# A graph layer's edge stages moved two pairs closer to their sums, with the third term of x1 . sh1 on ScalarE

## The chip, the core and the metric

The kernel runs on one core of a Trainium2 chip. The core has five engines with a queue each, worked off in order: TensorE (PE, matmuls; its weight loads are listed as PEld), VectorE (DVE), ScalarE (ACT), GpSimd (POOL) and SyncE (SP). They run side by side and meet through semaphores; POOL and SP here mostly issue DMA transfers. The metric is the time of one execution on the device, in microseconds (us); lower is better.

## The reference

A layer norm, a graph network, linear attention and a mixture of experts follow each other on 3125 nodes of width 512, all in float32. The change lies in the graph network, in what is done for each of 50,000 edges. A node's row is one scalar part of 128 channels (x0) and a vector part of 128 channels by 3 (x1). Cut to that:

```python
ip1 = jnp.einsum('eum,eum->eu', p1[edge_dst], p1[edge_src]) / 3.0
s0 = jnp.concatenate([pd0, pd0, ip1], axis=-1)
w = ssp(edge_attr @ W_f1) @ W_f2 * (ssp(s0 @ W_s1) @ W_s2)
w1, w2, w3, w4 = jnp.split(w, 4, axis=-1)
x0e, x1e = split_irreps(x[edge_src])
sh0, sh1 = (edge_sh[:, 0], edge_sh[:, 1:4])
out0 = w1 * x0e * sh0[:, None] + w4 * (jnp.einsum('eum,em->eu', x1e, sh1) / jnp.sqrt(3.0))
out1 = w2[:, :, None] * x0e[:, :, None] * sh1[:, None, :] + w3[:, :, None] * x1e * sh0[:, None, None]
out = jax.ops.segment_sum(merge_irreps(out0, out1), edge_dst, num_segments=N)
```

`ssp` is softplus less log 2. The einsum `eum,em->eu` is the x1 . sh1 of the title: a sum of three products, one for each component of the edge's direction.

## The kernel before, in words

First the kernel sorts the edges: each gets a record of 48 words (`recs`: its four sh values, source, destination, destination within its tile of 128 nodes, and the already known half of the hidden layer), laid out so that edges of one destination tile stand together. Node rows are written to two tables, `rows_d` (for the destination) and `rows_s` (for the source).

Then comes the edge stage, `run_pairs`. 128 edges are a tile, two tiles a pair, four tiles a quad (G = 4). 212 pairs, 106 quads, are always run; a further run follows only if the edges need more pairs. The stage's steps, with the lines that the profile names:

- `fetch` (POOL): per pair two gathers of `gd` (L710) and two of `gx` (L714). At the first pair of a quad SP loads the quad's records `rec2` (L699). There are 3 buffers of `gd`, 5 of `gx`, 6 of `rec2`, each holding a quad.
- `products` (DVE, L726): gd times gx for one pair, in two halves of a quad's `prod`.
- `turn` (PE, L734): 12 transposes that add up the three components of a quad into the PSUM tile `ps_ip`; `turn2` (ACT, L743) copies it to `ip`.
- `hidden` (PE): 24 small matmuls into `ps_h`, eight each from the records (L750), from `gd` (L755) and from `ip` (L760).
- `softplus` (ACT, L768, L771, L774, and L777 which copies the other half of `hT`), `softplus2` (DVE, L781, the second half of `hT`).
- `weigh`: for one pair PE makes `wa` (L799) and `wb` (L803) from the two halves of `hT`; ACT scales and copies `wa` to `wt` (L806 twice, L809); DVE multiplies by `wb` (L810). `wa` and `wb` have one buffer each.
- `dots` (ACT, L820) and `dots2` (DVE, L828 and L830): x1 . sh1 of a pair.
- `which` (DVE, L840): a matrix `one` that is 1 where an edge belongs to a node of the tile.
- `feats`: the edge's features `ft`: DVE L858, then six ACT instructions (L865) that scale one of its results, DVE L869, and DVE L874, which uses the dot product.
- `gather_up` (PE, L882): one.T times ft, added up over the pair in PSUM (eight matmuls in the profile); `keep_sums` (DVE, L891) adds it to the node tile's sums in `acc`.

POOL also copies a matrix of the experts' weights (`line_up`, L898) every sixth pair.

The order on PE, ACT, DVE and POOL is the program's own (`tc.manual_schedule`): what `run_pairs` writes down first stands first in that engine's queue, and waits there. The loop body is one pass for pair s. `due(a)` gives the quad whose first pair is s + a, so a step called with it comes in every second pass. `fetch` stands LEAD pairs ahead, `products` 7 and 6 ahead of the quad's first pair, `turn` 5, `hidden` 4, `softplus` 3, `softplus2` 2; `weigh`, `feats` and `dots2` work for pair s + 1, `dots` for s + 2, `gather_up` for s, `keep_sums` for s - 1. Most tiles that pass between the engines have two buffers, `ps_ip` and `ps_h` one.

Of the kernel before, what the change touches and what calls it, by code (L numbers as in the profile page):

```python
# [8 lines left out]
F32 = mybir.dt.float32  # L9
I32 = mybir.dt.int32  # L10
AF = mybir.ActivationFunctionType
ALU = mybir.AluOpType
# [4 lines left out]
P = 128  # L17
D = 512
MUL = 128
PR = 2  # L20
# [23 lines left out]
def gnn_mix_moe_kernel(ctx: ExitStack, tc: tile.TileContext, a: dict, out: bass.AP):  # L44
# [5 lines left out]
    nc = tc.nc  # L50
# [72 lines left out]
    with ExitStack() as c1:  # L123
# [313 lines left out]
        work = c1.enter_context(tc.tile_pool(name="work1", bufs=2, reuse_waits="tile"))  # L437
# [18 lines left out]
        for k0 in range(0, NPR, 44):  # L456
            ks = slice(k0, min(NPR, k0 + 44))
            k = ks.stop - k0
# [207 lines left out]
    with ExitStack() as c2:  # L666
        w = c2.enter_context(tc.tile_pool(name="w2", bufs=1, reuse_waits="tile"))
        gat = c2.enter_context(tc.tile_pool(name="gat", bufs=4, reuse_waits="tile"))
        work = c2.enter_context(tc.tile_pool(name="work2", bufs=2, reuse_waits="tile"))
# [24 lines left out]
        def fetch(q, k):  # L694

            Q = quads[q]
            if k == 0:
                Q.rec = gat.tile([P, G, REC], F32, name="rec2", bufs=6)
                loaded = nc.sync.dma_start(  # L699
                    Q.rec, recs[q * G * P : (q + 1) * G * P, :].rearrange("(p i) f -> p i f", i=G)  # L700
                )
                if q == 0:
                    for put in placed:
                        waits_for(loaded, put)

                Q.gd = gat.tile([P, G, HID + 3 * MUL], F32, name="gd", bufs=3)
                Q.gx = gat.tile([P, G, 3 * MUL + D], F32, name="gx", bufs=5)
            reci = Q.rec.bitcast(I32)
            for i in (2 * k, 2 * k + 1):
                nc.gpsimd.indirect_dma_start(  # L710
                    out=Q.gd[:, (i + 2) % G, :], out_offset=None, in_=rows_d[:, :],
                    in_offset=bass.IndirectOffsetOnAxis(ap=reci[:, i, 5:6], axis=0),
                )
                Q.last = nc.gpsimd.indirect_dma_start(  # L714
                    out=Q.gx[:, i, :], out_offset=None, in_=rows_s[:, :],
                    in_offset=bass.IndirectOffsetOnAxis(ap=reci[:, i, 4:5], axis=0),
                )

        def products(q, k):

            Q = quads[q]
            if k == 0:
                Q.prod = work.tile([P, G, 3 * MUL], F32, name="prod")
            x = slice(2 * k, 2 * k + 2)
            d = slice(2 - 2 * k, 4 - 2 * k)
            nc.vector.tensor_mul(Q.prod[:, d, :], Q.gd[:, d, HID:], Q.gx[:, x, : 3 * MUL])  # L726
# [13 lines left out]
        def turn2(q):  # L740
            Q = quads[q]
            Q.ip = work.tile([P, G, P], F32, name="ip")
            nc.scalar.copy(Q.ip, Q.ps_ip)  # L743
# [21 lines left out]
        def softplus(q):  # L765
            Q = quads[q]
            sp = work.tile([P, P], F32, name="sp")
            nc.scalar.activation(sp, Q.ps[:, 1, :], AF.Abs)  # L768
            if q * PR < NPR_MOST:
                with tc.issue_after(table.ins):  # L770
                    nc.scalar.activation(sp, sp, AF.Exp, scale=-1.0)  # L771
            else:
                nc.scalar.activation(sp, sp, AF.Exp, scale=-1.0)
            nc.scalar.activation(sp, sp, AF.Ln, bias=half, scale=0.5)  # L774
            Q.sp = sp
            Q.hT = work.tile([P, 2, P], F32, name="hT")
            nc.scalar.copy(Q.hT[:, 0, :], Q.ps[:, 0, :])  # L777

        def softplus2(q):
            Q = quads[q]  # L780
            nc.vector.scalar_tensor_tensor(  # L781
                Q.hT[:, 1, :], Q.ps[:, 1, :], 0.0, Q.sp, op0=ALU.max, op1=ALU.add
            )
# [3 lines left out]
        def parts(s):  # L787

            return quads[s // 2], (s % 2 * 2, s % 2 * 2 + 1)

        def weigh(s):

            Q, tiles = parts(s)
            R = pairs[s]
            wa = ps_w.tile([P, PR, D], F32, name="wa")
            wb = ps_w.tile([P, PR, D], F32, name="wb")
            for k, i in enumerate(tiles):
                r = slice(i * HID, (i + 1) * HID)
                nc.tensor.matmul(wa[:, k, :], Q.hT[r, 0, :], w_f2[r, :], start=True, stop=True)  # L799
            for k, i in enumerate(tiles):  # L800
                i = (i + 2) % G
                r = slice(i * HID, (i + 1) * HID)
                nc.tensor.matmul(wb[:, k, :], Q.hT[r, 1, :], w_s2[r, :], start=True, stop=True)  # L803
            R.wt = work.tile([P, PR, D], F32, name="wt")
            for k, i in enumerate(tiles):
                nc.scalar.activation(  # L806
                    R.wt[:, k, : 2 * MUL], wa[:, k, : 2 * MUL], AF.Copy, scale=Q.rec[:, i, 0:1]
                )
            nc.scalar.copy(R.wt[:, :, 2 * MUL :], wa[:, :, 2 * MUL :])  # L809
            nc.vector.tensor_mul(R.wt, R.wt, wb)  # L810

        def dots(s):

            Q, tiles = parts(s)
            R = pairs[s]
            R.dot = work.tile([P, 2, PR, MUL], F32, name="dot")
            x = Q.gx[:, :, 3 * MUL :]
            for c in (1, 2):
                for k, i in enumerate(tiles):
                    nc.scalar.activation(  # L820
                        R.dot[:, c - 1, k, :], x[:, i, c * MUL : (c + 1) * MUL], AF.Copy, scale=Q.rec[:, i, c : c + 1]
                    )

        def dots2(s):
            Q, tiles = parts(s)
            R = pairs[s]
            x = Q.gx[:, :, 3 * MUL :]
            nc.vector.tensor_add(R.dot[:, 0], R.dot[:, 0], R.dot[:, 1])  # L828
            for k, i in enumerate(tiles):
                nc.vector.scalar_tensor_tensor(  # L830
                    R.dot[:, 0, k, :], x[:, i, 3 * MUL :], Q.rec[:, i, 3:4], R.dot[:, 0, k, :],
                    op0=ALU.mult, op1=ALU.add,
                )

        def which(s):

            Q, tiles = parts(s)
            R = pairs[s]
            R.one = work.tile([P, PR, P], F32, name="one")
            nc.vector.tensor_tensor(  # L840
                R.one, lane.unsqueeze(1).to_broadcast([P, PR, P]),
                Q.rec[:, tiles[0] : tiles[1] + 1, 6:7].to_broadcast([P, PR, P]), op=ALU.is_equal,
            )
# [52 lines left out]
        def line_up(e, l):  # L896
            src = a["Wh"][e, l] if l < NL else a["Wo"][e]
            nc.gpsimd.dma_start(  # L898
                w_rows[l][e * P : (e + 1) * P, :].rearrange("p (k f) -> p k f", k=4),
                src.rearrange("(k p) f -> p k f", p=P),  # L900
            )

        def run_pairs(lo, hi):

            with tc.manual_schedule(
                engines={
                    mybir.EngineType.PE, mybir.EngineType.Activation, mybir.EngineType.DVE, mybir.EngineType.Pool
                }
            ):
                LEAD = 9  # L910
                for s in range(lo - LEAD, hi):
                    def due(ahead):

                        q, r = divmod(s + ahead, PR)
                        return [q] if r == 0 and lo <= q * PR < hi else []

                    if s + LEAD < hi:
                        fetch((s + LEAD) // PR, (s + LEAD) % PR)
                    if s >= lo and s % 6 == 0 and mats:
                        line_up(*mats.pop(0))  # L920
                    for q in due(2):
                        softplus2(q)
                    if lo <= s + 1 < hi:
                        which(s + 1)
                        dots2(s + 1)
                    for k in range(2):
                        for q in due(7 - k):
                            products(q, k)
                    if lo <= s - 1:
                        keep_sums(s - 1)  # L930
                    if lo <= s + 1 < hi:
                        weigh(s + 1)
                    for q in due(3):
                        softplus(q)
                    for q in due(5):
                        turn(q)
                    if lo <= s + 2 < hi:
                        dots(s + 2)
                    if lo <= s + 1 < hi:
                        feats(s + 1)  # L940
                    for q in due(5):
                        turn2(q)
                    if lo <= s:
                        gather_up(s)
                    for q in due(4):
                        hidden(q)
                keep_sums(hi - 1)

# [14 lines left out]
    with ExitStack() as c3:  # L963
# [17 lines left out]
        with tc.tile_pool(name="work3", bufs=2) as work:  # L981
# [107 lines left out]
            tiles = w.tile([P, NE], F32, name="tiles")  # L1089
# [308 lines left out]
```

## Time and profile before

| what | value |
|---|---|
| time, median of 3 runs | 2830.79 us (2830.1 to 2841.89) |
| the profiled execution: time / span | 2827.58 us / 2825.7 us |
| mean granted TensorE clock | 0.951 |
| busy share of the span: PE, PEld, DVE, ACT, POOL | 87%, 55%, 65%, 50%, 63% |
| first gather of the edge stage (L710) | 610.47 us |
| first L810 / first L882 | 651.58 us / 654.85 us |
| last L891 | 1913.47 us |

The profile is one execution. Its page gives each engine's busy time over the whole span; an average over stages with different limits. The edge stage takes about 1300 of the 2826 us, so the same shares are read again for a stretch inside it. In the timeline a line is a start in us, a duration, an engine and a source line; in brackets stands how long the engine had been idle and who released it. Instructions of one engine can overlap by a little, so the distance from one start to the next is what an instruction costs its queue.

### The profile page before, as it was taken

The numbers are of one execution on the slowest core, as the hardware profiler recorded it, in microseconds if no ns is written. First come the engines' busy times: TensorE is split into PE (matmuls) and PEld (weight loads), VectorE is DVE, ScalarE is ACT, GpSimd is POOL, SyncE is SP. The second block draws the span as 40 slices with busy tenths as digits, with TensorE's granted clock in tenths as the row PEclk, the third lists the DMA queues.
The fourth block names the chain that finished last, engine by engine and source line by source line (L and its number), as shares of the span: only waits on it lengthen the run. The fifth ranks groups of instructions, "written<-read, shape, count | busy, mean of one in ns | idle before, by whom it ended". The sixth has DMA issues, their size and how long they took to land. (4 is left out here: it accounts for less than half of the span.)

```text
span 2825.7 us, 45347 instructions
## 1 busy us (share of the span) xinstructions
PE 2472.2 (87%) x15014; PEld 1561.5 (55%) x15014; DVE 1838.4 (65%) x3758; ACT 1426.0 (50%) x4077; POOL 1771.1 (63%) x1756
## 2 busy tenths in 40 slices
PE   2676999208999999999999999996599999999998
PEld 2453466204444444444444444445488888888887
DVE  5878322028999999999999999995522222222222
ACT  1463321007888888888888888882311111111111
POOL 1778777777777777777777777721355555555553
PEclk7898999658999999999999999999799999999999
DMA  6663156338888888888888888835722723966452
GB/s 258 214 205 117 38 193 222 101 106 278 267 264 252 275 262 265 260 262 264 264 264 265 264 264 264 250 99 178 300 76 72 243 71 108 332 244 228 143 200 95
DMA packets 191656, 588.29 MB, mean 208 GB/s; under 512 B 54405, under 2 KB 79418, under 8 KB 179384
## 3 DMA queue, kind: packets, MB, share of 16 engines
q0 software_dynamic: 135216, 496.50, 54.3%
q1 hardware_dynamic: 49864, 82.54, 8.9%
q10 hardware_dynamic: 6336, 6.28, 0.7%
q8 instruction: 123, 2.02, 0.3%
q14 instruction: 117, 0.96, 0.1%
HBM read 635.54 MB, written 119.53 MB: 267 GB/s over the span
## 5 line engine op out<-in xcount | busy, mean ns | idle before, releaser
L882 PE MATMUL ps_s<-ft,one 128*128 128x512 f32 x1696 | 776.1, 600 | 40.5 <-DVE ft L869 40.5
L710 POOL DMA_INDIRECT gd<-rows_d,rec x424 | 460.1, 1085 | 181.4 <-issue 94.8
L882 PEld LDWEIGHTS ps_s<-ft,one 128*128 128x128 f32 x1696 | 306.0, 190 | 436.6 <-issue 256.0
L714 POOL DMA_INDIRECT gx<-rows_s,rec x424 | 416.4, 982 | 173.8 <-issue 96.3
L865 ACT ACTIVATE ft<-ft,rec 128x128 f32<-128x128 f32 x1272 | 395.0, 389 | 205.2 <-DVE ft L858 205.2
L396 POOL DMA_INDIRECT recs<-again,at_i x392 | 411.3, 1049 | 134.8 <-issue 108.8
L1273 ACT ACTIVATE h<-ps_f,bias 128x128 f32<-128x128 f32 x318 | 116.7, 367 | 622.0 <-PE ps_f L1260 611.9
L1260 PE MATMUL ps_f<-h,we 128*128 128x128 f32 x3392 | 401.6, 277 | 0.4 <-DVE h L1275 0.2
L1275 DVE TENSOR_SCALAR h<-ps_f,bias 128x128 f32<-128x128 f32 x318 | 111.1, 350 | 435.7 <-PE ps_f L1260 431.7
L1260 PEld LDWEIGHTS ps_f<-h,we 128*128 128x128 f32 x3392 | 387.0, 192 | 2.2 <-DVE h L1275 0.4
L1187 POOL DMA_INDIRECT we<-w_rows,w_at x212 | 214.5, 1012 | 225.8 <-PE ps_y L1291 99.5
L820 ACT ACTIVATE dot<-gx,rec 128x128 f32<-128x128 f32 x848 | 271.6, 397 | 0.0
L734 PE MATMUL ps_ip<-ident,prod 128*128 128x128 f32 x1272 | 165.9, 281 | 118.7 <-DVE prod L726 118.7
L810 DVE TENSOR_TENSOR wt<-wt,wb 128x1024 f32<-128x1024 f32 x212 | 257.0, 1212 | 0.3 <-ACT wt L809 0.3
L734 PEld LDWEIGHTS ps_ip<-ident,prod 128*128 128x128 f32 x1272 | 140.3, 143 | 198.5 <-issue 198.5
L803 PE MATMUL wb<-w_s,hT 32*128 32x512 f32 x848 | 240.3, 643 | 3.1 <-DVE wt L810 3.1
L799 PE MATMUL wa<-w_f,hT 32*128 32x512 f32 x848 | 239.4, 641 | 0.0
L726 DVE TENSOR_TENSOR prod<-gd,gx 128x768 f32<-128x768 f32 x212 | 201.6, 951 | 22.6 <-DMA gx<-rows_s,rec 22.6
L1260 PEld LDWEIGHTS ps_f<-xt,we 128*128 128x128 f32 x1696 | 200.0, 194 | 26.0 <-issue 23.7
L869 DVE TENSOR_TENSOR ft<-gx,wt 128x768 f32<-128x768 f32 x212 | 205.2, 968 | 0.0
L1260 PE MATMUL ps_f<-xt,we 128*128 128x128 f32 x1696 | 200.4, 277 | 0.7 <-ACT xt L1208 0.7
L1291 PE MATMUL ps_y<-we,h 128*128 128x512 f32 x424 | 196.1, 605 | 0.0
(301 smaller groups left out, 3545.6 us busy)
## 6 DMA issues: line engine op xcount, KB each, us to landing
w_rows<-in_Wh POOLq DMA_DIRECT2D x24, 1024.0 KB
rows_s<-r SPq DMA_DIRECT2D x24, 448.0 KB
recs<-zero POOLq DMA_DIRECT2D x10, 1056.0 KB
rec<-recs SPq DMA_DIRECT2D x106, 96.0 KB
lined<-rec SPq DMA_DIRECT2D x14, 672.0 KB
again<-lined POOLq DMA_DIRECT2D x14, 672.0 KB
w_rows<-in_Wo POOLq DMA_DIRECT2D x8, 1024.0 KB
gd<-rows_d,rec POOLq DMA_INDIRECT x424
```

What stands on the lines that cost most here:

```text
L396: put = nc.gpsimd.indirect_dma_start(out=recs[:, :], out_offset=bass.IndirectOffsetOnAxis(ap=at_i[:, t : t + 1], axis=0), in_=again[c][:, ...
L710: nc.gpsimd.indirect_dma_start(out=Q.gd[:, (i + 2) % G, :], out_offset=None, in_=rows_d[:, :], in_offset=bass.IndirectOffsetOnAxis(ap=reci ...
L714: Q.last = nc.gpsimd.indirect_dma_start(out=Q.gx[:, i, :], out_offset=None, in_=rows_s[:, :], in_offset=bass.IndirectOffsetOnAxis(ap=reci[ ...
L734: nc.tensor.matmul(ps[:, i, :], Q.prod[:, i, b * P : (b + 1) * P], ident, is_transpose=True, start=(b == 0), stop=(b == 2),)
L799: nc.tensor.matmul(wa[:, k, :], Q.hT[r, 0, :], w_f2[r, :], start=True, stop=True)
L803: nc.tensor.matmul(wb[:, k, :], Q.hT[r, 1, :], w_s2[r, :], start=True, stop=True)
L810: nc.vector.tensor_mul(R.wt, R.wt, wb)
L820: nc.scalar.activation(R.dot[:, c - 1, k, :], x[:, i, c * MUL : (c + 1) * MUL], AF.Copy, scale=Q.rec[:, i, c : c + 1])
L865: nc.scalar.activation(R.ft[:, k, D + c * MUL : D + (c + 1) * MUL], R.ft[:, k, 2 * D :], AF.Copy, scale=Q.rec[:, i, c : c + 1],)
L882: nc.tensor.matmul(R.ps, R.one[:, k, :], R.ft[:, k, m * D : (m + 1) * D], start=(k == 0 and m == 0), stop=(k == 1 and m == 1),)
L1187: nc.gpsimd.indirect_dma_start(out=dst, out_offset=None, in_=src, in_offset=bass.IndirectOffsetOnAxis(ap=at[:, j : j + 1], axis=0), bounds ...
L1260: nc.tensor.matmul(pss[f], ws[l][:, k, f * P : (f + 1) * P], h[:, k, :], start=(k == 0), stop=(k == 3))
```

## The change

Two edits, both in the edge stage.

First, the third product of x1 . sh1. `dots` lets ACT write all three products (six instructions a pair instead of four) into a `dot` tile with room for three, and `dots2` is two DVE additions over the pair instead of one addition and two multiply-adds.

Second, the order in `run_pairs`. LEAD goes from 9 to 7. `products` comes 5 and 4 pairs ahead of the quad's first pair (was 7 and 6), `turn` and `turn2` 3 (was 5), `hidden` 3 (was 4), `softplus` 2 (was 3). `softplus2` stays in the pass 2 ahead and goes from the head of the pass to behind `feats`; `softplus` now stands ahead of `turn`. `hidden` and `turn2` of a quad are now in one pass.

```diff
-            R.dot = work.tile([P, 2, PR, MUL], F32, name="dot")
+            R.dot = work.tile([P, 3, PR, MUL], F32, name="dot")
             x = Q.gx[:, :, 3 * MUL :]
-            for c in (1, 2):
+            for c in (1, 2, 3):
...
         def dots2(s):
-            Q, tiles = parts(s)
             R = pairs[s]
-            x = Q.gx[:, :, 3 * MUL :]
             nc.vector.tensor_add(R.dot[:, 0], R.dot[:, 0], R.dot[:, 1])
-            for k, i in enumerate(tiles):
-                nc.vector.scalar_tensor_tensor(
-                    R.dot[:, 0, k, :], x[:, i, 3 * MUL :], Q.rec[:, i, 3:4], R.dot[:, 0, k, :],
-                    op0=ALU.mult, op1=ALU.add,
-                )
+            nc.vector.tensor_add(R.dot[:, 0], R.dot[:, 0], R.dot[:, 2])
...
-                LEAD = 9
+                LEAD = 7
...
                         fetch((s + LEAD) // PR, (s + LEAD) % PR)
                     if s >= lo and s % 6 == 0 and mats:
                         line_up(*mats.pop(0))
-                    for q in due(2):
-                        softplus2(q)
                     if lo <= s + 1 < hi:
                         which(s + 1)
                         dots2(s + 1)
                     for k in range(2):
-                        for q in due(7 - k):
+                        for q in due(5 - k):
                             products(q, k)
                     if lo <= s - 1:
                         keep_sums(s - 1)
                     if lo <= s + 1 < hi:
                         weigh(s + 1)
+                    for q in due(2):
+                        softplus(q)
                     for q in due(3):
-                        softplus(q)
-                    for q in due(5):
                         turn(q)
                     if lo <= s + 2 < hi:
                         dots(s + 2)
                     if lo <= s + 1 < hi:
                         feats(s + 1)
-                    for q in due(5):
+                    for q in due(2):
+                        softplus2(q)
+                    for q in due(3):
                         turn2(q)
                     if lo <= s:
                         gather_up(s)
-                    for q in due(4):
+                    for q in due(3):
                         hidden(q)
```

## The prediction

> **What bounds the kernel now.** Three views, in this order. First the busy time of each engine by stretch (PE, PEld, DVE, ACT, POOL in us of 200, then the granted clock and the DMA share), for a stretch in the middle of the edge stage:
>
> ```profile
> 1300.00:1500.00 200.00, 193.85 (x1147) 90.50 (x1145) 197.65 (x353) 167.32 (x521) 143.38 (x141) 1.00 0.84 266
> ```
>
> VectorE (DVE) is busy 99%, TensorE (PE) 97% at full clock, ScalarE (ACT) 84%. Every stretch from 700 to 1900 us reads alike: 212 pairs, 106 quads, run in one rhythm. Second the timeline of that rhythm (start, duration, engine, line, what):
>
> ```profile
> 1303.29 0.40 PE L760 MATMUL ps_h<-ip,w_s1c 128*32 128x128 f32 x8
> 1303.62 0.70 PE L799 MATMUL wa<-w_f,hT 32*128 32x512 f32 x2
> ...
> 1306.12 0.81 ACT L806 ACTIVATE wt<-wa,rec 128x256 f32<-128x256 f32 x2
> 1306.83 0.57 ACT L809 COPY wt<-wa 128x512 f32<-128x512 f32 x1
> ...
> 1309.47 0.69 DVE L858 TENSOR_TENSOR ft<-wt,gx 128x512 f32<-128x512 f32 x1
> 1310.19 1.86 ACT L865 ACTIVATE ft<-ft,rec 128x128 f32<-128x128 f32 x6 [0.52 <-DVE ft L858]
> 1310.99 0.41 DVE L874 TENSOR_TENSOR ft<-wt,dot 128x256 f32<-128x256 f32 x1
> 1311.12 3.70 PE L882 MATMUL ps_s<-ft,one 128*128 128x512 f32 x8 [0.39 <-DVE ft L869]
> 1311.33 0.28 DVE L781 SCALAR_TENSOR_TENSOR hT<-ps_h,sp 128x128 f32<-128x128 f32 x1
> 1311.53 0.41 DVE L840 TENSOR_TENSOR one<-lane,rec 128x256 f32<-128x256 f32 x1
> 1311.86 0.41 DVE L828 TENSOR_TENSOR dot<-dot 128x256 f32<-128x256 f32 x1
> 1311.96 0.56 ACT L743 COPY ip<-ps_ip 128x512 f32<-128x512 f32 x1
> 1312.31 0.61 DVE L830 SCALAR_TENSOR_TENSOR dot<-gx,rec,dot 128x128 f32<-128x128 f32 x2
> 1312.84 0.95 DVE L726 TENSOR_TENSOR prod<-gd,gx 128x768 f32<-128x768 f32 x1
> 1313.71 0.68 DVE L891 TENSOR_TENSOR acc<-acc,ps_s 128x512 f32 x1
> 1314.31 1.21 DVE L810 TENSOR_TENSOR wt<-wt,wb 128x1024 f32<-128x1024 f32 x1
> 1315.55 0.69 DVE L858 TENSOR_TENSOR ft<-wt,gx 128x512 f32<-128x512 f32 x1
> 1316.16 0.95 DVE L869 TENSOR_TENSOR ft<-gx,wt 128x768 f32<-128x768 f32 x1
> 1317.03 0.41 DVE L874 TENSOR_TENSOR ft<-wt,dot 128x256 f32<-128x256 f32 x1
> ```
>
> DVE has no bracket of idle time on any line: it goes from one instruction to the next. Its L781 comes again at 1323.25, so a quad costs 11.92 us, and PE, ACT and POOL wait for DVE. Third, the end of the stage, where L726 has run out and DVE is relieved of 0.87 us a pair:
>
> ```profile
> 1871.59 3.70 PE L882 MATMUL ps_s<-ft,one 128*128 128x512 f32 x8 [0.34 <-DVE ft L869]
> ...
> 1883.07 3.70 PE L882 MATMUL ps_s<-ft,one 128*128 128x512 f32 x8
> ```
>
> The same matmuls, a quad apart, now without a wait: PE's own limit is 11.48 us.
>
> **The change, part by part.** I use start-to-start times, since neighbouring instructions overlap by some 0.07 us.
>
> *The third term.* On DVE the two L830 (0.53 from the first of them to L726) give way to one add of 128x256. Its nearest row is L840 (0.33 to the next) or L828, which is followed by an instruction that needs it (0.45); 0.33, because L726 follows and doesn't need it. DVE saves 0.20 a pair: 11.93 - 0.40 = 11.53 a quad, against PE's 11.48. ACT gets two more L820 a pair at 0.295 (six L865 start within 1.77), 1.18 a quad; it idles 1.38 + 0.52 = 1.90 now. Alone this would bring about 0.40 x 106 = 42 us.
>
> The Trainium skill ("Perfetto Trace Analysis", Identifying the Most-Contended Engine) says to optimize the engine of highest occupancy first. DVE's 99% agrees, and by that rule the sum would be 2827.6 - 42 = 2786 us. The rule doesn't ask what the new order makes each queue wait for, and the rows below speak against it.
>
> *The order.* What follows weighs more. Call the pass in which L734 (turn) is issued odd, the other even. In the new order PE's odd queue is L799/L803 (weights of the next pair), L734, L882, then L750, L755, L760 (hidden). L760 needs L743 of the same pass, which stands last on ACT: behind L806, L809, six L820 and six L865. Today L760 uses a copy made a pass earlier. In the even pass L781 now stands last on DVE, and the next L803 on PE needs it; today it is first, a pass ahead of its use. So all three queues form one ring per quad, which I walk with the rows above:
>
> 1. DVE from L781 to L810: 0.20 (to L840), 0.33, 0.45 (L828), 0.33 (new add), 0.87 (L726), 0.60 (L891) = 2.78
> 2. L810 to L858 1.24; L858 to the first L865 0.73; six L865 1.77 until L743 starts
> 3. L743 to L760: 0.67. The copy lasts 0.56; in the fill, at a lower clock, it starts at 627.54, L760's weights load at 628.18 and its matmuls start at 628.29, so between 0.64 and 0.75
> 4. L760 to L799 0.33 (1303.29 to 1303.62); L799 to L806 1.17 (661.34 to 662.51, where ACT waits for it); L806 to L809 0.71; L809 to L810 0.62 (663.24 to 663.86, where DVE waits for it)
> 5. L810 to L858 1.24, to L869 0.61, to L874 0.87, to L781 0.34
>
> The ring: 2.78 + 3.74 + 0.67 + 2.83 + 3.06 = 13.08 us a quad, 1.15 more than today's 11.93. For 106 quads +122 us. Queued behind the waiting L760 are the next L799 and L882; behind the waiting L803 the odd L734 and L882. PE's odd pass doesn't cover it: from L799 it has 1.08 of its own, 1.37 of L734, 3.53 of L882 and 0.46 of L750 and L755 (1303.62, 1304.70, 1306.07 and 1309.60 in the timeline; 1302.83 to 1303.29), 6.44, while L799 to the end of L743 needs 1.17 + 0.71 + 0.62 + 1.24 + 0.73 + 1.77 + 0.56 = 6.80. Nor is anything left to do between L882 and the late L803 of the odd pass.
>
> In the even pass ACT has a second route from L809 to L810 through softplus (1.57 with L809), six L820 (1.77), six L865 (1.77), L806 and L809 (1.33) = 6.44, against 6.46 over DVE. So of the third term's saving nothing more is to be had: ACT is level.
>
> *The lead.* Gathers start seven pairs ahead and L726 stands two pairs nearer, so gather to L726 stays two pairs; in the fill a gather lands some 3.4 us after its issue, well within 13. On POOL eight gathers at about 1.3 are 10.4 us a quad, L898's transfers 0.4: it keeps up. Buffers (three gd, five gx, six rec2) come free earlier relative to their gathers; POOL's present waits for L810 and L865 and SP's loads of rec2 hold nobody. If that cover went, a late landing would stall L726 for its lateness: today's six such stalls are all in the fill, 22.6 us together. The fill gets shorter: the first L810 comes after L726 of the fifth pair instead of the seventh, which started at 639.38 and 650.70, -11 us. At the end fewer passes run without L726: +1.
>
> *Sum*, against the profiled execution (span 2825.7, 1.9 around it, 2827.6 in all): +122 - 11 + 1 = +112, 2939.6. The median shown is 3.2 above that execution: 2943.
>
> *Bounds.* Below: step hand-overs cost nothing beyond the instructions themselves (0.11 in step 3, 0.04 to 0.05 at three others), 12.83 a quad, and the fill saves 15: 2827.6 + 95 - 15 + 3 = 2911. Above: all 24 hidden matmuls wait, not the last eight (0.80 instead of 0.33, the rows from L750 to L799), the new add costs 0.45, ACT adds 0.06: 13.73 a quad, +191, the fill saves 6: 3016. I take 13.08, as each of its steps has a row of its own.
>
> **The rivals.** *The ring is open and the DVE cut shows (other side).* If L743 found ACT free before the six L865, or L760's wait were covered, the ring would fall under DVE's 11.53. For it: DVE at 99%, and PE already idles for DVE. Against it: queues run in order and the deficit of 0.36 (6.80 against 6.44) and the late L803 recur in every quad. It decides from the point where the ring loses 1.15, as by the 1.77 of the L865. Price: -42 - 11 + 3 gives 2777.
>
> *The clock falls.* PE would idle 13.08 - 11.48 = 1.6 us a quad, 12%. From 130 to 160 us it was busy 77% at a clock of 0.83; there a quad would cost at least 11.48 / 0.83 = 13.8, over 3018. Against it: from 190 to 250 us 81% busy at 1.00, from 1930 to 1970 us 68% at 1.00. The low clocks stand beside long pauses.
>
> *The edits cancel.* A ring of 11.93 gives 2820 to 2830; nothing in the rows makes it so.
>
> **How the numbers follow.** The ring as walked has 0.87, the open ring 0.06, cancelling 0.02, a lower clock or a longer ring above 3015 0.05. The predicted time is the first's, 2943, and the range is its bounds with some room, 2900 to 3015; 1.3 in 10 is left out. The runs of before spread by 0.4%, so about 0.5% is what can be told from no change. Faster 0.06, same 0.02, slower 0.92.
>
> **What would show it.** In the middle of the stage a quad of 13.1 us; PE waiting at L760 for ACT L743, some 0.4 us a quad, and at L803 for DVE L781, some 1.2 us (together the 1.6 above); DVE waiting at L810 for ACT L809 once a quad, about 1 us; DVE busy about 11.53 / 13.08 = 88%; clock still 1.00; the first L810 about 11 us earlier. Wrong if L760 shows no wait, if DVE stays at 99%, or if PE's clock drops.

## The result and the profile after

The changed kernel takes 2957.77 us (median of 4 runs, 2953.07 to 2960.25) against 2835.84 us before (4 runs): a ratio of 1.0431 with a 95% interval of 1.0411 to 1.0452. It is 4.3% slower. The prediction was 2943 us in a range of 2900 to 3015. The profiled execution took 2959.99 us (span 2958.2 us), 132.4 us more than the one before.

The middle of the edge stage, busy time by stretch (PE, PEld, DVE, ACT, POOL, then clock, DMA share, GB/s):

```profile
1300.00:1500.00 200.00, 194.03 (x1027) 85.11 (x1025) 175.43 (x287) 169.59 (x533) 131.48 (x128) 1.00 0.76 238
```

DVE has fallen from 197.65 to 175.43 us of 200 (88%, the figure predicted). No engine has come nearer to being full in its place: ACT is busy 169.59 us (167.32 before), the clock is full, and the DMA share is lower. PE reads 97% as before although it does less (1027 matmuls instead of 1147 in the same 200 us); the timeline tells why. Line numbers past L826 are 5 to 6 lower in the new file: L865 is now L859, L858 L852, L869 L863, L874 L868, L882 L876, L840 L834; the two additions are L826 and L827.

```profile
1302.64 1.13 PE L799 MATMUL wa<-w_f,hT 32*128 32x512 f32 x4
...
1303.53 0.28 DVE L781 SCALAR_TENSOR_TENSOR hT<-ps_h,sp 128x128 f32<-128x128 f32 x1
1303.73 0.41 DVE L834 TENSOR_TENSOR one<-lane,rec 128x256 f32<-128x256 f32 x1
1303.95 1.13 PE L803 MATMUL wb<-w_s,hT 32*128 32x512 f32 x4 [0.19 <-DVE hT L781]
1304.06 0.42 DVE L826 TENSOR_TENSOR dot<-dot 128x256 f32<-128x256 f32 x1
1304.58 0.43 DVE L827 TENSOR_TENSOR dot<-dot 128x256 f32<-128x256 f32 x1
...
1304.92 0.95 DVE L726 TENSOR_TENSOR prod<-gd,gx 128x768 f32<-128x768 f32 x1
...
1305.01 1.53 PE L734 MATMUL ps_ip<-ident,prod 128*128 128x128 f32 x12
...
1306.39 1.22 DVE L810 TENSOR_TENSOR wt<-wt,wb 128x1024 f32<-128x1024 f32 x1
...
1307.64 0.69 DVE L852 TENSOR_TENSOR ft<-wt,gx 128x512 f32<-128x512 f32 x1
...
1308.37 1.86 ACT L859 ACTIVATE ft<-ft,rec 128x128 f32<-128x128 f32 x6 [0.37 <-DVE ft L852]
...
1310.13 0.56 ACT L743 COPY ip<-ps_ip 128x512 f32<-128x512 f32 x1
...
1310.75 0.43 PE L760 MATMUL ps_h<-ip,w_s1c 128*32 128x128 f32 x8 [0.20 <-ACT ip L743]
...
1311.11 0.70 PE L799 MATMUL wa<-w_f,hT 32*128 32x512 f32 x2
...
1312.28 0.84 ACT L806 ACTIVATE wt<-wa,rec 128x256 f32<-128x256 f32 x2 [1.58 <-PE wb L803]
...
1313.01 0.58 ACT L809 COPY wt<-wa 128x512 f32<-128x512 f32 x1
...
1313.63 1.22 DVE L810 TENSOR_TENSOR wt<-wt,wb 128x1024 f32<-128x1024 f32 x1 [0.85 <-ACT wt L809]
...
1316.70 0.28 DVE L781 SCALAR_TENSOR_TENSOR hT<-ps_h,sp 128x128 f32<-128x128 f32 x1
```

L781 comes again after 13.17 us, where it was 11.92; such a distance is called the rhythm below. The prediction's walk can be read off step by step:

| step | predicted | here |
|---|---|---|
| 1. L781 to L810 on DVE | 2.78 | 2.86 (the additions stand 0.52 apart, not 0.45) |
| 2. L810, L852, six L859, until L743 starts | 3.74 | 3.74 |
| 3. L743 to L760 | 0.67 | 0.62 |
| 4. L760, L799, L806, L809 to L810 | 2.83 | 0.36 + 1.17 + 0.73 + 0.62 = 2.88 |
| 5. L810 to L781 | 3.06 | 3.07 |
| a quad | 13.08 | 13.17 |

PE lost time in two places. From L750 to L799 the odd pass takes 1309.91 to 1311.11 = 1.20 us instead of 0.79 (L760 waits). And L799 with L803, eight matmuls that took 1.08 together before (start to the next L734), start at 1302.64 and hand over to L734 at 1305.01: 2.37 us. 11.48 + 0.41 + 1.29 = 13.18, the whole quad. The second loss is hardly to be seen as idle time: L799 goes ahead alone, so four matmuls run where eight ran side by side, and the engine counts as busy. The waits of the stretch from 700 to 1900 us (us in total, times, longest) show it only in the weight loads:

```profile
PEld wb L803 <- PE wa L799: 91.4, 91, 1.1
DVE wt L810 <- ACT wt L809: 77.8, 91, 1.1
...
PE ps_h L760 <- ACT ip L743: 18.9, 91, 0.4
PE wb L803 <- DVE hT L781: 18.7, 91, 0.3
```

### The profile page after: what moved, and what is told of

Its sections match the earlier page's. It is cut to its first block, busy times and chain, and to the rows that moved or that the text cites. A ratio compares the mean times of both kernels' runs of the same rounds, so it can differ in the third digit from the quotient of the medians.

```text
span 2958.2 us, 45457 instructions
## 1 busy us (share of the span) xinstructions
PE 2607.2 (88%) x15014; PEld 1591.5 (54%) x15014; DVE 1815.9 (61%) x3546; ACT 1552.1 (52%) x4501; POOL 1781.1 (60%) x1756
## 5 line engine op out<-in xcount | busy, mean ns | idle before, releaser
L876 PE MATMUL ps_s<-ft,one 128*128 128x512 f32 x1696 | 774.8, 599 | 1.1 <-DVE ft L863 1.1
L710 POOL DMA_INDIRECT gd<-rows_d,rec x424 | 435.9, 1028 | 347.0 <-DVE dot L826 236.5
L714 POOL DMA_INDIRECT gx<-rows_s,rec x424 | 447.5, 1055 | 129.2 <-issue 108.8
L876 PEld LDWEIGHTS ps_s<-ft,one 128*128 128x128 f32 x1696 | 305.5, 190 | 388.5 <-issue 307.3
L859 ACT ACTIVATE ft<-ft,rec 128x128 f32<-128x128 f32 x1272 | 393.4, 389 | 51.8 <-DVE ft L852 51.8
L820 ACT ACTIVATE dot<-gx,rec 128x128 f32<-128x128 f32 x1272 | 395.7, 395 | 0.0
L810 DVE TENSOR_TENSOR wt<-wt,wb 128x1024 f32<-128x1024 f32 x212 | 258.3, 1219 | 92.8 <-ACT wt L809 92.8
L806 ACT ACTIVATE wt<-wa,rec 128x256 f32<-128x256 f32 x424 | 175.7, 465 | 167.4 <-PE wb L803 167.4
L803 PE MATMUL wb<-w_s,hT 32*128 32x512 f32 x848 | 240.8, 641 | 25.1 <-DVE hT L781 25.1
L734 PE MATMUL ps_ip<-ident,prod 128*128 128x128 f32 x1272 | 164.6, 280 | 109.7 <-DVE prod L726 109.7
L734 PEld LDWEIGHTS ps_ip<-ident,prod 128*128 128x128 f32 x1272 | 139.2, 142 | 190.3 <-issue 190.3
L799 PE MATMUL wa<-w_f,hT 32*128 32x512 f32 x848 | 239.9, 642 | 1.3 <-ACT hT L777 1.3
L726 DVE TENSOR_TENSOR prod<-gd,gx 128x768 f32<-128x768 f32 x212 | 202.0, 953 | 15.9 <-DMA gx<-rows_s,rec 14.9
L863 DVE TENSOR_TENSOR ft<-gx,wt 128x768 f32<-128x768 f32 x212 | 201.8, 952 | 0.0
```

Source lines behind the costliest of these rows:

```text
L710: nc.gpsimd.indirect_dma_start(out=Q.gd[:, (i + 2) % G, :], out_offset=None, in_=rows_d[:, :], in_offset=bass.IndirectOffsetOnAxis(ap=reci ...
L714: Q.last = nc.gpsimd.indirect_dma_start(out=Q.gx[:, i, :], out_offset=None, in_=rows_s[:, :], in_offset=bass.IndirectOffsetOnAxis(ap=reci[ ...
L734: nc.tensor.matmul(ps[:, i, :], Q.prod[:, i, b * P : (b + 1) * P], ident, is_transpose=True, start=(b == 0), stop=(b == 2),)
L820: nc.scalar.activation(R.dot[:, c - 1, k, :], x[:, i, c * MUL : (c + 1) * MUL], AF.Copy, scale=Q.rec[:, i, c : c + 1])
L859: nc.scalar.activation(R.ft[:, k, D + c * MUL : D + (c + 1) * MUL], R.ft[:, k, 2 * D :], AF.Copy, scale=Q.rec[:, i, c : c + 1],)
L876: nc.tensor.matmul(R.ps, R.one[:, k, :], R.ft[:, k, m * D : (m + 1) * D], start=(k == 0 and m == 0), stop=(k == 1 and m == 1),)
```

## The experiments

The theory under test: two waits made by the order close a ring through the queues, and the ring's length is the rhythm. Rivals: ACT is short, with four activations more a quad; the shorter lead makes gathers late; or the waits are real but each simply costs its own length. The first four runs are one execution each and are read by their rhythm; the other four have 4 to 7 executions, set against 9 of the kernel before (median 2837.16 us).

**The order alone.** The changed kernel with the old `dots` and `dots2`:

```diff
-            R.dot = work.tile([P, 3, PR, MUL], F32, name="dot")
+            R.dot = work.tile([P, 2, PR, MUL], F32, name="dot")
-            for c in (1, 2, 3):
+            for c in (1, 2):
...
-            nc.vector.tensor_add(R.dot[:, 0], R.dot[:, 0], R.dot[:, 2])
+            for k, i in enumerate(tiles):
+                nc.vector.scalar_tensor_tensor(
+                    R.dot[:, 0, k, :], x[:, i, 3 * MUL :], Q.rec[:, i, 3:4], R.dot[:, 0, k, :],
+                    op0=ALU.mult, op1=ALU.add,
+                )
```

> The new order of the steps and LEAD 7, with the old two L820 terms on ScalarE and the multiply-adds on VectorE. My theory (a ring of waits through L743, L760, L799, L806, L810 and VectorE's pass sets the rhythm, 13.17 us a quad in the changed kernel): the ring gets longer by the dearer multiply-adds, 0.98 - 0.86 = 0.12 us once a quad, so 13.3 us a quad and some 2970 us. Rival (ScalarE, with four more activations a quad, is what the changed kernel is short of): ScalarE is relieved of 1.18 us a quad, so 12.0 us a quad and 2835 us at most.

Measured: 2963.02 us (the kernel before took 2833.25 beside these four runs), 13.29 us a quad. ACT is relieved (149.74 us busy of 200 instead of 169.59) and nothing is gained. The loss comes from the order; ACT's load is not its cause.

**The lead back at 9.**

```diff
-                LEAD = 7
+                LEAD = 9
```

> The changed kernel with LEAD 9 instead of 7: all gathers issued two pairs earlier, nothing else. My theory: gathers are hidden, 13.17 us a quad and 2955 us, within 6 us. Rival (gathers seven pairs ahead land late or POOL's waits hold them back): at least half of the loss comes back, under 2900 us.

Measured: 2966.1 us, 13.17 us a quad. That is 5 us over the bound given, but not from the edge stage: its last L885 starts at 2042.23 us, against 2043.71 with LEAD 7, and the rest of the span after it is 922.1 us against 914.5. The rhythm is the same to 0.01 us, so late gathers are not the cause. POOL's longer wait in the changed kernel (gd L710 behind DVE, 214.2 us in the stretch) is there with LEAD 9 too, 214.5.

**The copy early.** L743 ahead of `dots` and `feats`:

```diff
                     for q in due(3):
                         turn(q)
+                    for q in due(3):
+                        turn2(q)
                     if lo <= s + 2 < hi:
                         dots(s + 2)
...
-                    for q in due(3):
-                        turn2(q)
```

> The changed kernel with turn2 (L743's copy of ip) ahead of dots and feats in the pass, so that it no longer stands behind twelve activations. My theory: the ring through L743 is cut, and a second ring takes over, through L803's wait for L781: 0.42 + 1.06 + 1.37 + 3.53 + 0.79 + 1.17 + 0.73 + 0.62 + 1.25 + 0.61 + 0.87 + 0.34 = 12.76 us a quad, some 2915 us. Rival (each wait costs its own length): L760's delay of 0.41 us a quad goes, 2915 us too, so this run alone doesn't tell them apart; together with the next two it does.

Measured: 2913.3 us. The timeline has L781 12.77 us apart:

```profile
1305.62 0.28 DVE L781 SCALAR_TENSOR_TENSOR hT<-ps_h,sp 128x128 f32<-128x128 f32 x1
...
1306.05 1.13 PE L803 MATMUL wb<-w_s,hT 32*128 32x512 f32 x4 [0.19 <-DVE hT L781]
...
1307.11 1.53 PE L734 MATMUL ps_ip<-ident,prod 128*128 128x128 f32 x12
...
1308.48 3.60 PE L876 MATMUL ps_s<-ft,one 128*128 128x512 f32 x8
...
1312.01 0.43 PE L750 MATMUL ps_h<-ident,rec 128*32 128x128 f32 x8
...
1312.80 0.70 PE L799 MATMUL wa<-w_f,hT 32*128 32x512 f32 x2
...
1313.97 0.84 ACT L806 ACTIVATE wt<-wa,rec 128x256 f32<-128x256 f32 x2 [1.20 <-PE wb L803]
...
1315.32 1.22 DVE L810 TENSOR_TENSOR wt<-wt,wb 128x1024 f32<-128x1024 f32 x1 [0.45 <-ACT wt L809]
...
1318.39 0.28 DVE L781 SCALAR_TENSOR_TENSOR hT<-ps_h,sp 128x128 f32<-128x128 f32 x1
```

PE runs from L803 to L799 without a pause, so the first ring is cut, and yet only 0.40 us is won: now L781, L803, all of PE's odd pass, L799, and the way back over ACT and DVE to L781 are a ring of their own, 12.76 by the sum in the expectation.

**The softplus early.** L781 ahead of `feats` in its pass:

```diff
+                    for q in due(2):
+                        softplus2(q)
                     if lo <= s + 1 < hi:
                         feats(s + 1)
-                    for q in due(2):
-                        softplus2(q)
```

> The changed kernel with softplus2 (L781) ahead of feats, so that L803 need not wait for VectorE's L852, L863 and L868. My theory: the ring through L743 stays as it is, since L781 is one step of VectorE's pass wherever it stands: 13.1 to 13.2 us a quad, 2945 to 2960 us. Rival (each wait costs its own length): L803's 1.29 us a quad go, 11.9 us a quad and some 2822 us.

Measured: 2962.59 us, 13.13 us a quad. L799 and L803 run side by side again:

```profile
1306.18 0.43 PE L760 MATMUL ps_h<-ip,w_s1c 128*32 128x128 f32 x8 [1.46 <-ACT ip L743]
...
1310.19 0.28 DVE L781 SCALAR_TENSOR_TENSOR hT<-ps_h,sp 128x128 f32<-128x128 f32 x1
...
1311.23 0.70 PE L799 MATMUL wa<-w_f,hT 32*128 32x512 f32 x2
1311.25 0.70 PE L803 MATMUL wb<-w_s,hT 32*128 32x512 f32 x2
...
1323.33 0.28 DVE L781 SCALAR_TENSOR_TENSOR hT<-ps_h,sp 128x128 f32<-128x128 f32 x1
```

The 1.29 us that this freed on PE appear at L760, where the wait went from 0.20 to 1.46 us. PE's busy time fell from 194 to 178 us of 200 at the same pace. A wait of more than a microsecond, repeated in every quad, was worth nothing by itself. The rival that counts each wait at its length expected 2822.

**Both early.** The two moves together:

> The changed kernel with both moves at once: turn2 ahead of dots, softplus2 ahead of feats. My theory: both rings are cut and VectorE's own work binds again: 11.92 less 2 x (0.98 - 0.86) = 11.68 us a quad, 25 us off the kernel before, and 10 more for the shorter fill: 2790 to 2810 us. Rival (each wait costs its own length): 13.17 - 0.41 - 1.29 = 11.47, some 2780 us; and if a third wait takes over, 12 us a quad or more and over 2835 us.

Measured: 2800.22 us, a ratio of 0.9868 (0.9822 to 0.9914) to before. The moves alone brought 0.40 and 0.04 us a quad, together 1.5: L781 stands 11.63 to 11.70 us apart in most quads, DVE is busy 98% and PE reads 100%:

```profile
1307.53 0.28 DVE L781 SCALAR_TENSOR_TENSOR hT<-ps_h,sp 128x128 f32<-128x128 f32 x1
...
1319.16 0.28 DVE L781 SCALAR_TENSOR_TENSOR hT<-ps_h,sp 128x128 f32<-128x128 f32 x1
...
1300.00:1500.00 200.00, 200.00 (x1161) 95.48 (x1160) 195.60 (x326) 189.66 (x601) 139.56 (x144) 1.00 0.85 270
```

The rival's sum (some 2780) lies below the run's lowest execution, 2789.4; its other half, a third wait, didn't come.

**The term alone.** The kernel before with the first edit only (its diff is the upper part of the change):

> The kernel before with the third term alone: six L820 a pair on ScalarE, two additions on VectorE, old order, LEAD 9. My theory: VectorE sets the rhythm, 11.68 us a quad, 25 us less than before, some 2810 us. The prediction's own figure was 42 us less, with 0.33 us for the added addition; the profile of the changed kernel has 0.52 us from L826 to L827. Rival (ScalarE is short): slower than before.

Measured: 2811.41 us, ratio 0.9918 (0.9894 to 0.9941). Alone the edit is a gain of about 25 us (17 to 30 by the interval). Its two additions stand 0.51 to 0.52 us apart here too (1303.78 and 1304.29).

**The gap filled.** As both early, with L834 issued between the two additions:

```diff
             nc.vector.tensor_add(R.dot[:, 0], R.dot[:, 0], R.dot[:, 1])
+            which(s)
             nc.vector.tensor_add(R.dot[:, 0], R.dot[:, 0], R.dot[:, 2])
...
                     if lo <= s + 1 < hi:
-                        which(s + 1)
                         dots2(s + 1)
```

> As the run with both moves, and L834 (which) issued between the two additions, so that the second need not follow the first at once. If the 0.52 us is a wait of the second addition for the first one's result, VectorE saves 0.18 us a pair more, 11.32 us a quad, and TensorE's 11.48 binds: 20 us less than the run with both moves, some 2780 us. If an addition simply costs that much after another, no gain.

Measured: 2781.85 us, ratio 0.9805 (0.9773 to 0.9836), the fastest of all. In the timeline (the additions are L826 and L828 here, `which` L835) each follows the one before after 0.33 us:

```profile
1302.42 0.42 DVE L826 TENSOR_TENSOR dot<-dot 128x256 f32<-128x256 f32 x1
1302.75 0.42 DVE L835 TENSOR_TENSOR one<-lane,rec 128x256 f32<-128x256 f32 x1
1303.09 0.42 DVE L828 TENSOR_TENSOR dot<-dot 128x256 f32<-128x256 f32 x1
1303.42 0.95 DVE L726 TENSOR_TENSOR prod<-gd,gx 128x768 f32<-128x768 f32 x1
```

That an addition simply takes so long behind another one is ruled out by a pair of independent additions outside the edge stage, in the trace of the changed kernel. They too start 0.34 us apart:

```profile
155.85 0.42 DVE L367 TENSOR_TENSOR kfs<-kfs,kf 128x256 f32<-128x256 f32 x1
156.19 0.69 DVE L352 TENSOR_TENSOR so_far<-so_far,b_add 128x512 f32<-128x512 f32 x1
```

So the 0.52 us was the second addition waiting for the first one's result. L734 now comes every 11.46 us in 90 of 105 quads, 0.02 from PE's limit as read off the end of the old stage (11.48). At this pace L726 now and then waits for a gather: 19 times, 17.5 us in all, from 700 to 1860 us. From the first gather to the last sum the profiled execution takes 1255.5 us here and 1267.7 with both moves alone, 12 less and not the expected 20; the rest of the difference lies outside the stage.

**The same in the old order.** The kernel before with the term and L840 between the additions:

> The old order and LEAD 9 with the third term and L840 (which) between the two additions. My theory: 11.48 us a quad, TensorE's limit, 45 us less than before, some 2790 us, and about 10 us more than the run with both moves and the same edit, as the fill stays long.

Measured: 2791.58 us, ratio 0.9839 (0.9803 to 0.9875). The medians are 10 us apart, as expected. The first L810 does come 31.8 us after the first gather in the run with both moves (614.26 to 646.02), 41.3 here (612.52 to 653.83). But the profiled executions don't put the difference down to this shorter fill: from the first gather to the last L886 they take the same, 1255.5 us (to 1869.71) and 1256.9 us (to 1869.45), and what follows the stage is 909.1 us there and 917.8 here. L726 waits only 1.6 us for gathers here, instead of 17.5. The two intervals overlap as well, so that the new order gains anything over the old one once the gap is filled isn't shown.

## Why the prediction was right, and where not

**The sign and the mechanism** were right. The order closes a ring through L743, L760, L799, L806, L809, L810 and DVE's pass; its length, 13.08 by rows of the old trace, was measured as 13.17. The order alone gives 13.29, and LEAD 9 again 13.17.

**The size** came out 20 us short of the profiled execution (112 against 132.4). The ring's term was 0.09 us a quad too small, 9.5 us in 106 quads, almost all of it step 1: the added addition was priced at 0.33 us and L828 before it at 0.45, but the second of two additions on the same tile starts 0.52 after the first. The fill saved 9.8 us up to the first L810 (31.3 us after the first gather instead of 41.1; 11 predicted), and the second L810 gave 2.9 of it back, waiting 3.15 us for L809. The rest of the stage cost 1.5 more than the +1 allowed for its end; in it stand 26 quads that took 0.07 to 0.24 us longer than 13.17, 3.0 us together. The remaining 5.5 lie outside the stage: the first gather came 3.2 us later (613.68 instead of 610.47), and what follows the stage was 2.3 us longer (914.5 instead of 912.2). The range had no room at its upper end: the bound worked out for it was 3016, the range ends at 3015.

**L803's wait was put in the wrong place.** The prediction counted it as part of the one ring and gave its 1.2 us and L760's 0.4 together as the price. The size of both was right (1.29 and 0.41), but the walk itself never passed through L803: it went from L781 to L810 on DVE. Taking L803's wait away left the rhythm where it was (13.13). It belongs to a second, shorter ring of 12.77, which is only seen when the first is cut.

**The open-ring rival had the wrong point of decision.** It said that the ring falls under DVE's limit if L743 finds ACT free before the six L865. With exactly that arranged the time is 2913 us, since the second ring takes over; two cuts are needed. Once both are made the rival's world is there, at 2800 and not 2777, as the term is worth 25 us and not 42: the added addition costs DVE 0.52 + 0.34 us with the one before it, not 0.45 + 0.33.

**Covers.** Gathers were hidden as said (0.01 us a quad between LEAD 7 and 9), but only at the slow rhythm: at 11.46 us a quad the new order with LEAD 7 waits 17.5 us for them, the old one with LEAD 9 1.6. No run there separates the lead from the order. ACT was named level, with no room; in the order alone it is relieved and the quad grows by 0.12, DVE's dearer multiply-adds, as that reading implies. The clock stayed at 1.00 through waits of up to 1.46 us in every quad.

**The occupancy rule.** The Trainium skill ("Perfetto Trace Analysis", Identifying the Most-Contended Engine) says to work on the engine of highest occupancy first. For the term it held: with DVE at 99%, taking work from DVE brought 0.8%. On the order that rule says nothing, and 2786 us, the sum by it, was 172 us off. The section's caution that matmul busy share is not a good measure of how close PE is to its peak showed up here in a special form: 97% in both kernels, at 11.92 and 13.17 us a quad.

**What was looked for.** PE's wait at L760 shows as idle time of 0.20 us, though the path from L750 to L799 lost 0.41. The wait at L803 shows as 0.19, though 1.29 was lost. DVE's wait at L810 for L809 is there, 0.85 once a quad.

## What to carry to other kernels

When steps are moved in queues that run in order, write down for each moved step who must now wait in the same pass, and walk from that wait through every queue until you are back: the longest such ring is the rhythm, whatever the busy shares say. A wait is worth only what its ring exceeds the next ring by, so two waits may be worth far more together than one by one (here 0.40 and 0.04 us a quad alone, 1.5 together). Before giving up a slow change, undo its edits one at a time: here one of the two was a gain, and two moved calls took away the other's whole loss.

## What the runs showed that was not expected

Two DVE instructions of 128x256 of which the second needs the first one's result start 0.52 us apart when both are additions into one tile, and 0.45 when the second is the multiply-add L830 (128x128). Independent ones start 0.33 to 0.34 us apart, and so do three when an independent one stands between the two additions. Filling the gap took 18 us off the median (2800.22 to 2781.85).

A late operand can hide in a busy engine. L799 and L803 use different quarters of PE's rows; issued together all eight took 1.08 us to the next L734; apart, four take 1.13 and the other four 1.13 again. That matmuls on different row groups run at once is what the Trainium skill says too ("TensorE: Matmul & The Clock Gate", Part 3: Packing small matmuls); the trace adds that the loss of it shows as PE being busy, so the busy share has to be read with the count of matmuls in a stretch: 1027 in 194.03 us here, 1033 in 178.03 us at the same pace in the run with the softplus early, where they are side by side again.
